# The gate stage of a four-layer convolution kernel, rewritten as one hand-ordered stream over rows of 8x8 blocks

## The chip, the cores and the metric

The kernel runs on one core of a Trainium2 chip. The metric is the device time of one launch in microseconds (us), as a median over runs. The core has five engines that work side by side and meet through semaphores: TensorE (PE, matrix products; its weight loads are listed as PEld), VectorE (DVE), ScalarE (ACT, functions by table), GpSimd (POOL) and SyncE (SP, which here only issues DMAs). Each takes its own instructions strictly in the order in which they stand.

## The reference

The input `x` is (2, 128, 128, 128) in float32: two images of 128 channels, 128 rows and 128 columns. Four layers follow each other. Layer 0 and layer 2 are a 3x3 convolution, a small state-space scan over every pixel, a group norm and a residual. Layer 3 is a basic block of two convolutions with signs as weights. Layer 1, which the change is about, is this:

```python
g = x.reshape(B, GROUP, c, hh, WINDOW, ww, WINDOW)          # GROUP = 4, c = 32, WINDOW = 8
g = g.transpose(0, 1, 3, 5, 2, 4, 6).reshape(B * GROUP * hh * ww, c, 64)
sq = jnp.sum(g * g, axis=-1)
gram = jnp.einsum('ncw,ndw->ncd', g, g)
dist2 = jnp.maximum(sq[:, :, None] + sq[:, None, :] - 2.0 * gram, 0.0)
density = jnp.exp(-0.5 * dist2).mean(axis=-1)               # one value per channel and 8x8 block
y = jax.nn.relu(einsum('bchw,oc->bohw', density, w1) + b1)  # 128 -> 32 channels
y = einsum('bchw,oc->bohw', y, w2) + b2                     # 32 -> 128 channels
attn = upsample_bilinear_ac(jax.nn.sigmoid(y) + 0.5, 8)     # 16x16 blocks -> 128x128 pixels
return x * attn
```

So each 8x8 block of each channel is compared with the same block of the 32 channels of its group, the densities make a gate for each block and channel, and the gates, spread bilinearly over the pixels, multiply `x`. An output row needs the gates of the block rows just above and below it.

## The kernel before

The three stages that matter stand one behind the other: `_mamba` for layer 0, `_gates`, and `_mamba` for layer 2. Channels (or states) lie on the 128 partitions.

`_mamba` issues its work by hand: every piece gets a due time, the pieces are sorted, and they are recorded inside `tc.manual_schedule`, so each engine's order is that of the list. Its scan over tokens (L451, L469, L478, L479, L483) takes most of the program's time. It writes its output `y`, not yet normalised, to DRAM, and statistics of it to `stats`.

`_gates` goes over the 32 slabs of 8 rows (16 for each image b), each 128 x 1024 elements. The scheduler of the language decides each engine's order there, from the order of the source and its own priorities. `_norm` turns the statistics of both images into a scale and a shift, ahead of all slabs. Then, for a slab:

- `load` (L633, L635): two DMAs of 512 KB bring `y` and the layer's input; ACT applies SiLU (L636), POOL adds both in a block order, giving `x` (L638), which stays in SBUF in one of 21 buffers (`nh + 5`).
- `turn`: eight transposes on PE (L652) into PSUM tile `pt`; DVE copies it to `xt` (L654), ACT squares it to `xq` (L656) and squares `x` to `sq` (L659); DVE sums and scales to `nsq` (L661, L662).
- `density`: PE forms the Gram matrices in PSUM tile `pg` (L671 with `xq`, then L681 with `xt`); DVE adds `nsq` (L689), POOL clamps (L695), ACT takes the exponential (L696).
- `total`: DVE sums to `dens` (L700).

When all 16 slabs of an image have their `dens`, `gain(b)` makes the gates of the whole image: PE (L707), ACT ReLU (L709), and four times PE (L717, L718), ACT sigmoid (L719) and DVE add (L720). Only then can `apply` run for that image, slab by slab: PE spreads the gates over the pixels (L738), from gates that lie in four groups of 32 partitions, `k // 2` choosing the group, so two neighbouring segments mostly share one; DVE multiplies with `x` (L747), in two pieces where a segment boundary cuts the slab; ACT's queue issues the store (L751). The loop interleaves one `apply` of image 0 with one `turn` of image 1; the 16 applies of image 1 come behind everything.

In PSUM, one tag (`pt`, two buffers of three banks) serves `turn`, `apply` and `gain`, and `pg` has one buffer of two banks. The first instruction of layer 2 is a memset of its row band (L193), whose SBUF space the gate stage used, so it waits for the last store of the gate stage; then come the band's load (L198) and the convolution (L328).

The functions that the diff touches and their callers:

Of the kernel before, what the change touches and what calls it, by code (L numbers as in the profile page):

```python
# [31 lines left out]
P = 128  # L32
# [59 lines left out]
def _place(k):  # L92


    q = k // 2
    return k % 2 + 2 * (q // 4), q % 4


def _upsampling(H):

    _, fy = _bilinear(H)
    ix, fx = _bilinear(P)
    wx = np.zeros((P // WIN, P), np.float32)
    wx[ix, np.arange(P)] = 1.0 - fx
    wx[ix + 1, np.arange(P)] += fx
    segs = _segments(H)
    up = np.zeros((4, 2, P // WIN, 4, max(e - a for _, a, e in segs), P), np.float32)
    for k, a, e in segs:
        n, g = _place(k)
        for h in range(a, e):  # L110
            up[g, 0, :, n, h - a] = (1.0 - fy[h]) * wx
            up[g, 1, :, n, h - a] = fy[h] * wx
    return up.reshape(P, 4, -1)
# [488 lines left out]
def _gates(tc, src, w, con, y, stats, wm, b1, up, dst, H):  # L602

    nc = tc.nc
# [3 lines left out]
    nwin = nh * nw  # L608
    segs = _segments(H)
    with tc.tile_pool(name="dg", bufs=2) as dp, tc.tile_pool(name="dg1", bufs=1) as sp, tc.tile_pool(  # L610
        name="ps_t", bufs=2, space=PSUM
    ) as pst, tc.tile_pool(name="ps_g", bufs=1, space=PSUM) as psg:

        def wide():
            return pst.tile([P, 3 * ROWS, P], F32, tag="pt", name="pt")

        class Small:


            def tile(self, shape, dtype, tag=None, name=None):  # L620
                return wide().rearrange("p a b -> p (a b)")[: shape[0], : shape[1]]

        norm = [_norm(nc, sp, Small(), w, con, stats, b) for b in range(B)]
        ct = sp.tile([P, 4, up.shape[2]], F32, tag="ct", name="ct")

        dens = [sp.tile([P, nh, 2, npair], F32, tag=f"dens{b}", name="dens") for b in range(B)]
        held, live, gains = {}, {}, {}

        def load(b, y0):

            rows = slice(y0 * WIN, (y0 + 1) * WIN)
            g = dp.tile([P, WIN, P], F32, tag="g", name="g", bufs=4)
            nc.sync.dma_start(out=g, in_=y[b][:, rows, :])  # L633
            xr = dp.tile([P, WIN, P], F32, tag="xr", name="xr", bufs=4)
            nc.sync.dma_start(out=xr, in_=src[b][:, rows, :])  # L635
            nc.scalar.activation(g, g, AF.Silu, bias=norm[b][1], scale=norm[b][0])  # L636
            x = held[b, y0] = dp.tile([P, nw, WIN, WIN], F32, tag="x1", name="x1", bufs=nh + 5)
            nc.gpsimd.tensor_tensor(by_row(x), by_row(xr, False), by_row(g, False), ALU.add)  # L638
# [6 lines left out]

        def turn(b, y0):

            x = held[b, y0].rearrange("p x r w -> p (x r w)")

            pt = wide()[:, :npair, :]  # L650
            for k in range(npair):
                nc.tensor.transpose(pt[:, k, :], x[:, k * P : (k + 1) * P], con["ident"])  # L652
            xt = dp.tile([P, npair, P], F32, tag="xt", name="xt")
            nc.vector.tensor_copy(xt, pt)  # L654
            xq = dp.tile([P, npair, P], F32, tag="xq", name="xq")
            nc.scalar.activation(xq, pt, AF.Square)  # L656

            sq = dp.tile([P, nw, WIN * WIN], F32, tag="sq", name="sq", bufs=1)
            nc.scalar.activation(sq.rearrange("p x r -> p (x r)"), x, AF.Square)  # L659
            nsq = dp.tile([P, nw], F32, tag="nsq", name="nsq")  # L660
            nc.vector.tensor_reduce(nsq, sq, AX.X, ALU.add)  # L661
            nc.vector.tensor_scalar_mul(nsq, nsq, -0.5)  # L662
            live[b, y0] = xt, xq, nsq

        def density(b, y0):
            xt, xq, nsq = live.pop((b, y0))

            pg = psg.tile([P, 2, 512], F32, tag="pg", name="pg")
# [19 lines left out]
            kk = dp.tile([P, 2, npair, CG], F32, tag="kk", name="kk", bufs=3)  # L688
# [6 lines left out]
            nc.gpsimd.tensor_scalar_min(kk, kk, 0.0)  # L695
            nc.scalar.activation(kk, kk, AF.Exp)  # L696
            live[b, y0] = kk

        def total(b, y0):
            nc.vector.tensor_reduce(dens[b][:, y0], live.pop((b, y0)), AX.X, ALU.add)  # L700

        def gain(b):

            den = sp.tile([P, nh, npair, 2], F32, tag="den", name="den")
            nc.vector.tensor_scalar_mul(den, dens[b].rearrange("p y a k -> p y k a"), 1.0 / CG)
            p1 = wide().rearrange("p a b -> p (a b)")[:CG, :nwin]
            nc.tensor.matmul(p1, lhsT=wm["w1"], rhs=den.rearrange("p y k a -> p (y k a)"), start=True, stop=True)  # L707
            hid = sp.tile([CG, nwin], F32, tag="hid", name="hid")
            nc.scalar.activation(hid, p1, AF.Relu, bias=b1)  # L709
            p2 = wide()[:, :4, :]  # L710
            gt = gains[b] = sp.tile([P, 4, P], F32, tag="gain", name="gain")
            for n in range(4):
                at = (n % 2 + n // 2 * WIN) * nw
                m = min(P, nwin - at) // 32 * 32
                if m <= 0:
                    continue
# [39 lines left out]
        for n in range(-4, N + 2):  # L756
            if ready:
                apply(*ready.pop(0))
# [237 lines left out]
```

## Time and profile before

| | us |
|---|---|
| median of 9 runs | 7870.99 (7850.73 to 7903.14) |
| time of the profiled execution | 7870.99 |
| its span in the trace | 7869.2 |
| busy PE / DVE / ACT / POOL over the span | 6556.4 / 6837.2 / 4291.1 / 5518.9 |
| last scan output of layer 0 on DVE (L511) | 3321.2 |
| first transpose of the gate stage (L652) | 3341.85 |
| last transpose of the gate stage | 3560.8 |
| last multiplication (L747) begins | 3638.3 |
| memset of layer 2's band (L193) | 3643.28 |

The page's busy shares are means over stages of different kinds. The gate stage is about 320 us of 7869, some 4% of the span, so it must be read from windows of its own. In a group's row, the first number behind the bar is busy time, the second the mean duration of one instruction in ns, and then follows the idle time of the engine just ahead of such instructions with what ended it. A row's `x` counts instructions; a float32 matmul appears as two. `PEclk` is the granted clock of TensorE as a share of full speed.

### The profile page before, as it was taken

The page shows a single profiled execution, that of the slowest core. Times are in us where ns is not written, and L with a number is a line of the kernel's source. Part 1 is how long each engine was busy: PE and PEld are TensorE (multiplying, and loading weights), DVE is VectorE, ACT ScalarE, POOL GpSimd, SP SyncE. Part 2 cuts the span into 40 slices and gives each one's busy share as a digit, 9 for nine tenths or more (in the row PEclk, how much of TensorE's full clock was granted, in tenths as well). Part 3 has the DMA queues.
Part 4 walks back from the last instruction along what each step waited for, and adds up shares of the span by engine and source line. Part 5 has one row for each costly group of instructions (what it writes and reads, how often), then busy time and mean ns, then how long its engine had stood idle before and what let it go on. Part 6 is the DMA issues. An engine that isn't in the chain of part 4 may idle for free. (4 is left out here: it accounts for less than half of the span.)

```text
span 7869.2 us, 86792 instructions
## 1 busy us (share of the span) xinstructions
PE 6556.4 (83%) x29412; PEld 2221.6 (28%) x29412; DVE 6837.2 (87%) x6360; ACT 4291.1 (55%) x4835; POOL 5518.9 (70%) x1810
## 2 busy tenths in 40 slices
PE   7888888888888888778888888888888888878893
PEld 2222222222222222253222222222222222223341
DVE  5999999999999999863999999999999999963454
ACT  5566565666666656482656666666666656621112
POOL 5777877777778778552777777777777778843330
PEclk8999999999999999766999999999999999989996
DMA  7999999999999999753999999999999999955204
GB/s 197 244 252 248 255 249 247 251 253 248 253 250 250 250 244 256 210 181 124 244 251 249 251 249 247 250 249 247 253 250 246 249 250 251 250 157 139 69 0 163
DMA packets 573435, 1765.42 MB, mean 224 GB/s; under 512 B 85536, under 2 KB 239680, under 8 KB 458176
## 3 DMA queue, kind: packets, MB, share of 16 engines
q1 hardware_dynamic: 530496, 1709.54, 84.0%
q10 hardware_dynamic: 42496, 50.34, 1.8%
q8 instruction: 234, 3.83, 0.2%
q14 instruction: 209, 1.71, 0.1%
HBM read 1549.82 MB, written 209.72 MB: 224 GB/s over the span
## 5 line engine op out<-in xcount | busy, mean ns | idle before, releaser
L451 POOL TENSOR_TENSOR h<-ur,bcr 128x2048 f32<-128x2048 f32 x896 | 4059.6, 4537 | 1273.0 <-DMA bcr<-sb 1058.2
L478 DVE TENSOR_TENSOR set<-set,h 128x1024 f32<-128x1024 f32 x1792 | 2194.3, 1224 | 308.3 <-ACT set L469 303.6
L479 DVE TENSOR_TENSOR r<-set,bcr 128x1024 f32<-128x1024 f32 x1792 | 2194.5, 1225 | 61.5
L469 ACT ACTIVATE set<-set 128x1024 f32<-128x1024 f32 x1792 | 1745.7, 1007 | 866.1 <-PE set L460 851.7
L483 DVE TENSOR_TENSOR h<-set,h 128x1024 f32<-128x1024 f32 x1536 | 1866.1, 1215 | 22.3 <-POOL h L451 22.1
L460 PE MATMUL set<-dt,rep 32*128 32x512 f32 x7168 | 1406.5, 676 | 100.2 <-DVE h L483 94.2
L498 PE MATMUL ys<-r,ct 128*32 128x512 f32 x7168 | 1173.2, 636 | 35.5 <-DVE r L479 35.3
L328 PE MATMUL one<-band,conv 128*128 128x512 f32 x2304 | 1085.7, 608 | 24.0 <-DMA band<-in_x_dram 11.6
L828 PE MATMUL m<-comb,u 128*128 128x512 f32 x1536 | 689.5, 610 | 88.6 <-DVE Y L842 52.1
L406 PE MATMUL one<-xc,keep 128*64 128x512 f32 x1024 | 330.0, 728 | 468.0 <-ACT xc L363 362.6
L460 PEld LDWEIGHTS set<-dt,rep 32*128 32x128 f32 x7168 | 406.2, 193 | 998.5 <-issue 465.5
L328 PEld LDWEIGHTS one<-band,conv 128*128 128x128 f32 x2304 | 408.3, 190 | 673.9 <-issue 598.9
L489 PE MATMUL ys<-t,ct 128*128 128x512 f32 x512 | 325.8, 723 | 251.7 <-DVE v L511 250.2
L357 ACT ACTIVATE xc<-one,keep 128x512 f32<-128x512 f32 x256 | 176.0, 688 | 518.2 <-PE one L355 513.4
L498 PEld LDWEIGHTS ys<-r,ct 128*32 128x32 f32 x7168 | 181.1, 112 | 933.7 <-issue 764.2
L828 PEld LDWEIGHTS m<-comb,u 128*128 128x128 f32 x1536 | 297.1, 195 | 480.2 <-issue 457.7
L426 PE MATMUL one<-prod,ct 128*128 128x512 f32 x512 | 284.8, 639 | 114.5 <-POOL prod L418 78.0
L355 PE MATMUL one<-y,w_in 128*128 128x512 f32 x512 | 343.7, 760 | 5.8 <-ACT xc L357 3.1
L380 POOL TENSOR_TENSOR u<-dt,xc 128x1024 f32<-128x1024 f32 x128 | 302.7, 2365 | 51.1 <-ACT dt L374 51.1
L469 ACT ACT_TABLE_LOAD x252 | 323.3, 1283 | 4.5
L370 PE MATMUL one<-xc,w_dt 128*128 128x512 f32 x512 | 316.7, 703 | 4.1 <-ACT bc L413 4.1
L433 POOL TENSOR_TENSOR t<-t,xc 128x1024 f32<-128x1024 f32 x128 | 302.4, 2362 | 10.0
(136 smaller groups left out, 5751.1 us busy)
## 6 DMA issues: line engine op xcount, KB each, us to landing
ur<-su SPq DMA_DIRECT2D x896, 896.0 KB, 11.6
bcr<-sb SPq DMA_DIRECT2D x896, 448.0 KB, 11.8
ur<-su SPq DMA_DIRECT2D x896, 128.0 KB, 11.2
su<-u SPq DMA_DIRECT2D x1024, 64.0 KB, 3.1
sb<-bc SPq DMA_DIRECT2D x256, 224.0 KB, 2.8
bcr<-sb SPq DMA_DIRECT2D x896, 64.0 KB, 11.1
y<-o SPq DMA_DIRECT2D x128, 256.0 KB, 9.5
band<-in_x_dram SPq DMA_DIRECT2D x28, 640.0 KB, 10.9
```

Source lines behind the costliest of these rows:

```text
L328: nc.tensor.matmul(py.rearrange("p (r w) -> p r w", r=ROWS), lhsT=w["conv"][:, tap, :], rhs=xb[:, r + kh : r + kh + ROWS, kw : kw + P], st ...
L355: nc.tensor.matmul(p, lhsT=w[("in", "z")[i]][:, g, :], rhs=s["y"], start=True, stop=True)
L406: nc.tensor.matmul(p[g * NQ * DS : (g + 1) * NQ * DS, :], lhsT=w[("xb", "xcm")[i]], rhs=s["xc"][:, g, :], start=True, stop=True,)
L451: nc.gpsimd.tensor_tensor(b, s["ur", t], s["bc", t][:, 0].unsqueeze(1).to_broadcast([P, NJ, NS]), ALU.mult)
L460: nc.tensor.matmul(a[j // 2][:, j % 2, :], lhsT=w["rep"][r, q, :], rhs=s["dt"][r, g, :], start=True, stop=True, tile_position=(r.start, 0),)
L469: nc.scalar.activation(x, x, AF.Exp)
L478: nc.vector.tensor_tensor(pt, pt, s["h", t - 1][:, js, :], ALU.mult)
L479: nc.vector.tensor_tensor(s["r", t][:, js, :], pt, s["bc", t - 1][:, 1].unsqueeze(1).to_broadcast([P, 2, NS]), ALU.mult)
L483: nc.vector.tensor_tensor(s["h", t][:, js, :], pt, s["h", t][:, js, :], ALU.add)
L489: nc.tensor.matmul(s["ys", g], lhsT=con["ident"], rhs=s["t1"][:, g, :], start=True, stop=False)
L498: nc.tensor.matmul(s["ys", g][a : a + NQ * DJ, :], lhsT=red[:, q, :], rhs=r[:, j, :], start=False, stop=(q == NQ - 1), tile_position=(0, a),)
L828: nc.tensor.matmul(m[:, i], lhsT=u[:, i, kw, :], rhs=v[:, i, :, kw : kw + P], start=(kw == 0), stop=(kw == 2),)
```

## The change

`_gates` is rewritten as one stream over the 32 slabs, inside `tc.manual_schedule`. The source loops over steps n, and in step n every piece of work is issued for slab n minus its own distance ("lag"). The whole-image gate is gone. A slab's `hide` makes the hidden values of its own row of 16 blocks and puts them in a row of `hidden[b]`, `gate` makes the gates of four rows of blocks at once (twice, in partitions 0 to 63 and 64 to 127), the sigmoid is ACT's exponential with a sum, a reciprocal and a sum on DVE (128 x 128), and `spread` fills a slab with two matmuls of 64 x 512, one from each half of the partitions. The multiplication is one instruction for a slab. The store moves from ACT's queue to SP's. The second image's `_norm` is issued in step 10, in front of that step's `gram`, instead of ahead of the stage. The upsampling constant grows from 128 x 4608 to 128 x 8192 elements. `x1` has 15 buffers instead of 21; `pt` has two of two banks; `pg`, `one` and `two` have one each. SiLU and POOL's addition are issued two slabs at a time, as are the loads.

```diff
+            s["xt"] = dp.tile([P, npair, P], F32, tag="xt", name="xt")
+            nc.vector.tensor_copy(s["xt"], pt)
+            s["xq"] = dp.tile([P, npair, P], F32, tag="xq", name="xq")
+            nc.scalar.activation(s["xq"], pt, AF.Square)
+            s["sq"] = dp.tile([P, nw, WIN * WIN], F32, tag="sq", name="sq")
+            nc.scalar.activation(s["sq"].rearrange("p x r -> p (x r)"), x, AF.Square)
...
-            den = sp.tile([P, nh, npair, 2], F32, tag="den", name="den")
-            nc.vector.tensor_scalar_mul(den, dens[b].rearrange("p y a k -> p y k a"), 1.0 / CG)
-            p1 = wide().rearrange("p a b -> p (a b)")[:CG, :nwin]
-            nc.tensor.matmul(p1, lhsT=wm["w1"], rhs=den.rearrange("p y k a -> p (y k a)"), start=True, stop=True)
-            hid = sp.tile([CG, nwin], F32, tag="hid", name="hid")
-            nc.scalar.activation(hid, p1, AF.Relu, bias=b1)
...
+        def hide(b, y0):
+            s = live[b, y0]
+            s["ph"] = psg.tile([CG, nw], F32, tag="one", name="ph")
+            nc.tensor.matmul(
+                s["ph"], lhsT=wm["w1"], rhs=s.pop("den").rearrange("p a k -> p k a"), start=True, stop=True
+            )
+
+        def hide_relu(b, y0):
+            nc.scalar.activation(hidden[b][:, y0 + 1, :], live[b, y0].pop("ph"), AF.Relu, bias=b1, scale=1.0 / CG)
+
+        def gate(b, y0):
+            s = live[b, y0]
+            p = s["pz"] = psg.tile([P, P], F32, tag="two", name="pz")
+            h = hidden[b][:, y0 : y0 + 4, :].rearrange("p y x -> p (y x)")
+            for a in range(0, P, P // 2):
+                nc.tensor.matmul(p[a : a + P // 2, :], lhsT=h, rhs=wm["w2"], start=True, stop=False)
+                nc.tensor.matmul(p[a : a + P // 2, :], lhsT=wm["one"], rhs=wm["b2"], start=False, stop=True)
+
+        def gate_exp(b, y0):
+            s = live[b, y0]
+            s["e"] = dp.tile([P, P], F32, tag="e", name="e")
+            nc.scalar.activation(s["e"], s.pop("pz"), AF.Exp, scale=-1.0)
+
+        def gain(b, y0):
+            e = live[b, y0]["e"]
+            nc.vector.tensor_scalar_add(e, e, 1.0)
+            nc.vector.reciprocal(e, e)
+            nc.vector.tensor_scalar_add(e, e, 0.5)
+
+        def spread(b, y0):
+            s = live[b, y0]
+            pu = s["pu"] = pst.tile([P, 2 * ROWS, P], F32, tag="pt", name="pu")
+            for n in range(2):
+                q = slice(n * P // 2, (n + 1) * P // 2)
+                nc.tensor.matmul(
+                    pu[:, n * ROWS : (n + 1) * ROWS, :].rearrange("p r w -> p (r w)"),
+                    lhsT=s["e"][q, :],
+                    rhs=weights[q, y0, :],
+                    start=True,
+                    stop=True,
+                )
...
+        stages = (
+            (3, density),
+            (6, hide_relu),
+            (8, gate_exp),
+            (1, norms),
+            (2, distance),
+            (0, turn),
+            (4, total),
+            (9, gain),
+            (10, apply),
+            (10, keep),
+            (1, gram),
+            (7, gate),
+            (5, hide),
+            (9, spread),
+        )
+        E = mybir.EngineType
+        with tc.manual_schedule(engines={E.PE, E.Activation, E.DVE, E.Pool, E.SP}):
+            for n in range(-6, N + 11):
+                if n % 2 == 0:
+                    for m in range(max(n + 4, 0), min(n + 6, N)):
+                        load(*order[m])
+                    for m in range(max(n + 2, 0), min(n + 4, N)):
+                        residual(*order[m])
+                for lag, stage in stages:
+                    if stage is gram and 0 <= n + 6 < N and order[n + 6][1] == 0:
+                        b = order[n + 6][0]
+                        norm[b] = _norm(nc, sp, psg, w, con, stats, b)
+                    if 0 <= n - lag < N:
+                        stage(*order[n - lag])
```

## The prediction

> **What bounds the kernel now.** I read the page first: DVE is busy 87% of the span, PE 83%, but both shares come from the two scan stages, which the change leaves alone. So I cut the gate stage out with windows: loading and first slabs, the part in which image 0 is also spread, and the rest in which only image 1 is spread.
>
> ```profile
> core 0: us, PE busy (x) PEld busy (x) DVE busy (x) ACT busy (x) POOL busy (x), PEclk, DMA share, GB/s
> ...
> 3342.00:3452.00 110.00, 66.08 (x2592) 53.74 (x2592) 71.19 (x85) 106.64 (x102) 70.46 (x36) 0.72 0.62 212
> 3452.00:3576.00 124.00, 107.44 (x2378) 67.74 (x2378) 82.60 (x106) 68.55 (x74) 49.70 (x27) 0.68 0.37 129
> 3576.00:3643.00 67.00, 58.52 (x106) 29.32 (x106) 21.33 (x28) 2.85 (x6) 0.00 (x0) 0.50 0.33 134
> ```
>
> Three limits follow each other. For 110 us ACT is busy 97%: 18 transposes in 110 us, 6.1 us a slab. For 124 us PE is busy 87%, 14 slabs at 8.9 us. For the last 67 us nothing but PE and DVE works, in turns, at half clock. The chain of waits for the second window, then two rows of it for the third:
>
> ```profile
> DVE o L747 <- PE pt L738: 16.0, 11, 3.2
> PEld pt L652 <- DVE o L747: 15.6, 6, 3.0
> ```
>
> ```profile
> POOL band L193 <- DMA x<-o: 70.7, 1, 70.7
> DVE o L747 <- PE pt L738: 34.2, 18, 4.1
> ```
>
> Multiplication and spread alternate through the two PSUM buffers; in the tail DVE waits 34.2 us for PE, and the next layer (POOL's band) waits for the last store. The tail exists only because an image's gates wait for its last density. The groups of the second window give the durations at its clock:
>
> ```profile
> L738 PE MATMUL pt<-ct,gain 32*128 32x512 f32 (+3 forms) x88 | 44.8, 636 | 2.3 <-DVE o L747 2.2
> ...
> L681 PE MATMUL pg<-xt 64*32 64x32 f32 x1920 | 24.7, 230 | 2.0 <-issue 2.0
> ...
> L652 PE MATMUL pt<-ct,x 128*128 128x128 f32 x112 | 23.7, 373 | 9.3 <-DVE o L747 8.6 <-ACT xq L656 0.7
> ...
> L671 PE MATMUL pg<-xq,ct 64*32 64x256 f32 x240 | 16.9, 566 | 1.8 <-DVE kk L689 1.8
> ```
>
> Per slab on PE: transposes 23.7/14 = 1.69 us, L671 16.9/15 = 1.13, L681 24.7/15 = 1.65, spread 44.8/16 = 2.8.
>
> **The change part by part.** The sum starts at ACT's first L656, at 3345.3 before, and ends with the last L747, at 3638.6 before. The profiled run took 7870.99 us, the median of the nine runs, 1.8 us more than its span; I subtract from both alike. What follows is counted from the order of the instructions on each engine.
>
> *Start.* The g loads lose a wait: SP stood 5.3 us at the load of `keep` (L235, for the second image's norm), with all loads queued behind; it now comes after the first store. But the constant ahead of them grows from 2304 KB, which took 8.5 us, to 4096 KB: 12 to 15 us from 3321.3, estimated at that rate and at the 440 GB/s of its best moments. Before its first squares ACT now also takes SiLU of slabs 2 and 3, so it waits for seven loads of 512 KB, 1.25 us each at that rate. Start: 3345, within 3 us. The second norm overlapped the first before; now it stands in step 10, between `apply` and the next sum on DVE and between `turn` and `gram` on PE. The whole chain took 3326.0 to 3331.8 for both; I charge 5.5 us.
>
> *Table loads.* SiLU two at a time and exponentials otherwise: 14 loads for SiLU and 15 for the exponential where the page has 21 and 22, and none for the sigmoid (3). One takes 1.283 us. ACT per slab: 1.24 (SiLU) + 1.01 + 1.05 + 0.63 + 1.28 (one load a slab) + 0.28 (L719's row, for the new exponential) + 0.2 (ReLU on 32 x 16, the 0.20 of L208) = 5.7 us.
>
> *Steps 0 to 8* (nothing is spread). ACT sets them: 9 x 2.06 (two squares), 8 SiLU 9.9, 6 exponentials 3.8, 7 table loads 9.0, the rest 1: 42 us; with 3 for waits, 45.
>
> *Spread on PE.* Before, 88 instructions for 16 slabs, mostly in one group of 32 rows, one behind the other. Now four for a slab, two in each half of the rows. The scan shows what row groups do:
>
> ```profile
> 3282.21 1.14 PE L460 MATMUL set<-dt,rep 32*128 32x512 f32 x8
> ...
> 3570.11 3.77 PE L738 MATMUL pt<-ct,gain 32*128 32x512 f32 x4
> ```
>
> Eight of the same size in four row groups took 1.14 us, where four in turn took 3.77 (at half clock; 1.89 at 3565). The row at half clock in row groups is 2.08 (3309.97). So 1.1 to 2.1, and 2.5 (4 x 0.636) if the halves do not overlap; I take 1.6. The Trainium skill, "TensorEngine Tiling (Array Packing)", Key Properties, speaks against it: changing the tiling mode drains the array, and each step here changes among full, 64 x 32, 64 x 64 and 64 x 128. The trace has such changes too (L652 to L671: 3506.01 after 1.90 us of transposes), and no gap beyond 0.3 us stands there; I add nothing. Four changes at 0.3 would add 1.2 us a step.
>
> *Gates.* Eight instructions of 128 columns and two of 16. L717 and L718 ran four in 1.2 us at half clock; in two column halves 0.85 to 2.4 for the eight, I take 0.9, and 0.1. PE per step: 1.69 + 1.13 + 1.65 + 1.0 + 1.6 = 7.1 us.
>
> *DVE.* The new gain: two sums of 128 x 128 (L720, median 0.23) and a reciprocal. The trace has reciprocals of 128 x 1 only (L209, 160 ns, against 155 of L207). From below: L747's row of 128 x 128, 0.28. From above: the skill's "VectorE: DVE Perf Modes" (Walkthrough) says that the reciprocal divides iteratively with a repeat count of 8; 128 x 8 at its 0.96 GHz is an estimated 1.07, with a fixed part 1.2. One column cannot tell these apart. I take 1.2; with 0.28 the step's loop below is 0.9 shorter, and the PE sum (7.1) rules: 11 us less in all.
>
> These operations also meet POOL:
>
> ```profile
> 3405.03 2.37 POOL L638 TENSOR_TENSOR x<-xr,g 128x1024 f32<-128x1024 f32 x1 [1.25 <-ACT g L636]
> 3405.79 1.64 DVE L662 TENSOR_SCALAR nsq<-nsq 128x16 f32<-128x16 f32 x1
> ```
>
> A scaling of 16 columns, 174 ns in the median, lasts until POOL's addition ends. Its mean is 490 and its maximum 2377: about 0.3 us each. "SBUF — State Buffer" (two separate sides) has the rule: a shared port pair is held for a whole instruction. By the mean, two sums add 0.6 a step; by the rule's worst, each waits 2.37. DVE per step: 1.22 + 1.22 + 0.49 + 0.69 + 0.68 + 0.46 + 1.2 + 0.6 + 1.22 = 7.8 by durations, some 7.1 since a following instruction starts up to 0.09 early.
>
> *Steps 9 to 31.* The lags take most waits out, but one loop is left. From the waits, `spread` takes the PSUM buffer that the same step's `turn` filled, so it waits for the copy `xt` and for `xq`, and it waits for `gain`, which stands behind `xt` and `total` on DVE; the next `turn` stands behind `spread` on PE. Loop: 1.69 + 1.22 + 0.68 + 0.46 + 1.2 + 0.6 + 1.6, and 0.2 for semaphores = 7.6 us. That is above the sums of PE (7.1), DVE (7.1) and ACT (5.7), so a late `gain` holds back `spread`, and behind it on PE every transpose. 23 steps: 175 us.
>
> *Tail.* Steps 32 to 41: one with `gram`, about 6 us, six with gates and spread at half clock (1.2 + 2.1), three shorter at 2.6: 33 us, where the old tail took 62.6. Spreads then alternate in the two buffers, so DVE and PE overlap.
>
> *Stores.* Their issue goes from ACT to SP, 0.33 us each behind a wait for `apply`; behind it are loads that have two steps (15 us) against 7.6 to land. They get late by part of a step at most. Without that slack a late store would move loads one for one. POOL's clamp now stands behind two additions (4.7 us) in every second step; its reader comes a step later. The last store lands after 4.7 us as before, and layer 2's band waits for it as before.
>
> Sum: 3345 + 45 + 175 + 5.5 + 33 = 3603.5 against 3638.6: 35 us less. Span 7834, median 7836.
>
> **The rivals.** (1) PE runs warmer. The clock was 0.68 in the second window with PE held up by DVE in between; if the closer stream brings full speed (transposes were 1.09 at 3391), the step falls to 6.2, by ACT and DVE: 23 x 1.4 = 32 us less, 7804. For it: 0.94 in the scan. Against: 0.72 and 0.68 in the gate stage, both with PE far from idle. (2) The distance is only on paper: PE stays at half clock (transposes 1.97, Gram 2.75, gates 1.3, spread 2.5, with drains) and the loop adds its waits, 8.9 us a step as before. Then only head, fill and tail gain: 23 x 1.3 = 30 us back, 7866. (3) Slower: the port. In every second step POOL runs two additions and a clamp back to back, some 6.2 us, and each of the two sums, perhaps the reciprocal too, can fall into it and wait up to 2.37. All sit on the loop. It decides from 9.1 us a step (35/23 = 1.5 over 7.6); at 10.4, 1.4 us more in each of two operations, it gives 23 x 2.8 - 35 = 29 us more, 7900. Against it: L662's median is the undisturbed 174 ns.
>
> **How the numbers follow.** 0.3% (24 us) is about what a measurement of this kernel can tell from no change. Forecast 0.60, 7 to 8.2 us a step, 7822 to 7850, a tenth of it above 7847; rival 1 0.22; rival 2 0.11; rival 3 0.07. Faster 0.54 + 0.22 = 0.76, same 0.06 + 0.11 = 0.17, slower 0.07. The range goes from 7798 (6.2 a step with a shorter start and tail) to 7866: it leaves out part of rivals 1 and 2, and 3.
>
> **What would show it.** Right: transposes 7 to 8 us apart in steps 9 to 31, spreads of four in 1.1 to 2.1, PE waiting at `spread` for `gain`, ACT's table loads at 29, last multiplication near 3603. Wrong: a reciprocal far from 1.2, sums of 128 x 128 above 1 us in the mean (rival 3), a clock above 0.9 (rival 1), spreads above 2.5, or a span that differs outside the gate stage by over 10 us.

## The result and the profile after

The changed kernel took 7851.92 us in the median of its first 11 runs (7834.58 to 7871.27), against 7870.38 for the kernel before in the same comparison: a ratio of 0.9975, with a 95% interval of 0.9963 to 0.9987. Repeated beside other kernels it gave 0.9965 (0.9952 to 0.9977). So it is faster by a quarter to a third of one per cent, 19 to 27 us, where 35 were predicted; the 24 us that the prediction took as the least that can be told from no change lie between the two. Its profiled span is 7844.1 us, 25.1 less.

Between profiles the end of layer 0, which no kernel here touches, lies anywhere from 3307.6 to 3335.5 us. What follows is therefore measured inside one trace, as the length of the stage: from layer 0's last scan output on DVE (L504 of the changed kernel, L511 before) to the memset of layer 2's band (L186, before L193). Before it was 3643.28 - 3321.23 = 322.1 us; after, 3616.35 - 3320.22 = 296.1 us, and 295.1 in the repeat. Such lengths come from one profile of each kernel.

The stage again in windows. The columns are those of the prediction's first fence: window and length, busy us (and instructions) of PE, PEld, DVE, ACT and POOL, granted clock, DMA share, GB/s. The windows are the steps before anything is spread, steps 9 and 10, the steady steps, and the tail:

```profile
3341.00:3398.00 57.00, 31.31 (x1249) 25.96 (x1250) 30.85 (x37) 41.81 (x46) 35.61 (x18) 0.80 0.61 222
3398.00:3425.40 27.40, 16.41 (x337) 10.80 (x337) 16.26 (x34) 15.24 (x20) 10.77 (x7) 0.50 0.28 104
3425.40:3579.00 153.60, 115.08 (x3488) 77.52 (x3486) 139.26 (x187) 105.56 (x141) 71.64 (x38) 0.89 0.49 181
3579.00:3614.00 35.00, 28.41 (x248) 12.43 (x246) 28.31 (x45) 4.69 (x15) 2.97 (x2) 0.55 0.37 151
```

In the third row DVE is busy 91% of the time, PE 75%, and PE's clock is 0.89 where the longest window before had 0.68. The tail is 35 us instead of 67, with DVE and PE both busy 81% of it: they overlap now. In the second row no engine is busy for more than 60% of the time: 27 us for two steps, at half clock.

The chain of waits for the third row:

```profile
DVE xt L648 <- PE pt L646: 13.9, 9, 3.9
...
PE pg L678 <- issue: 9.6, 8, 2.0
PE pg L668 <- DVE kk L690: 9.3, 12, 0.8
...
PE pu L745 <- DVE e L737: 6.2, 6, 2.1
```

DVE waits for one thing only, the transposes, 13.9 us in nine places; PE waits in turn for DVE's gain and distance, and 9.6 us for nothing that this view shows ("issue"; the repeat below names it). For the fourth row, the waits that answer to the last two lines shown before:

```profile
POOL band L186 <- DMA x<-o: 30.6, 1, 30.6
...
DVE o L756 <- PE pu L745: 4.3, 5, 1.1
```

DVE's 34.2 us of waiting for the spread have become 4.3. The band still waits for the last store, but for 30.6 us and not 70.7. The groups of the steady steps (21 of them):

```profile
L745 PE MATMUL pu<-up,e 64*128 64x512 f32 x86 | 30.6, 786 | 11.2 <-DVE e L737 6.2 <-ACT sq L652 5.0
L678 PE MATMUL pg<-xt 64*32 64x32 f32 x2688 | 29.8, 202 | 9.6 <-issue 9.6
...
L646 PE MATMUL pt<-ct,x 128*128 128x128 f32 x168 | 28.7, 327 | 0.0
...
L736 DVE RECIPROCAL e<-e 128x128 f32<-128x128 f32 x21 | 20.0, 953 | 0.7
...
L668 PE MATMUL pg<-xq,ct 64*32 64x256 f32 x336 | 15.7, 434 | 9.3 <-DVE kk L690 9.3
...
L737 DVE TENSOR_SCALAR e<-e 128x128 f32<-128x128 f32 x21 | 12.6, 601 | 0.7
...
L735 DVE TENSOR_SCALAR e<-e 128x128 f32<-128x128 f32 x21 | 9.4, 450 | 0.0
```

The reciprocal costs 0.953 us. The two sums take 0.450 and 0.601 in the mean, where the shortest of each takes 0.216 and 0.226: waits for the port of 0.23 + 0.37 = 0.6 us a step.

From turn to turn, the fill (first xq to step 9) took 51.7 us, step 9 12.6, step 10 15.0, and steps 11 to 31 7.35 each, (3572.32 - 3425.39)/20. That mean hides a pattern of two. A step in which ACT takes two SiLUs and POOL two additions (the even ones) lasts 8.0 us, the other 6.5 (medians; 7.6 and 6.5 in the repeat). Most experiments below are read in this pair.

The trace shows what an even step waits for (starts and durations in us; the lines between are left out):

```profile
3495.11 4.70 POOL L637 TENSOR_TENSOR x<-xr,g 128x1024 f32<-128x1024 f32 x2 [8.36 <-ACT g L635]
...
3497.03 0.55 DVE L735 TENSOR_SCALAR e<-e 128x128 f32<-128x128 f32 x1
...
3497.62 0.95 DVE L736 RECIPROCAL e<-e 128x128 f32<-128x128 f32 x1
...
3498.60 1.29 DVE L737 TENSOR_SCALAR e<-e 128x128 f32<-128x128 f32 x1
...
3499.76 1.50 POOL L696 TENSOR_SCALAR kk<-kk 128x512 f32<-128x512 f32 x1
```

POOL's two additions end near 3497.5 and at 3499.81. The first sum is released by the one (0.55 instead of 0.22), the second by the other (1.29, ending at 3499.89). The reciprocal between them runs beside an addition at its full speed.

### The profile page after: what moved, and what is told of

The parts are those of the page before. It is cut to its first block, busy times and chain, and to the rows that moved or that the text cites. A ratio compares the mean times of both kernels' runs of the same rounds, so it can differ in the third digit from the quotient of the medians.

```text
span 7844.1 us, 87434 instructions
## 1 busy us (share of the span) xinstructions
PE 6499.7 (83%) x29648; PEld 2198.1 (28%) x29648; DVE 6873.4 (88%) x6432; ACT 4279.4 (55%) x4873; POOL 5519.6 (70%) x1812
## 5 line engine op out<-in xcount | busy, mean ns | idle before, releaser
L491 PEld LDWEIGHTS ys<-r,ct 128*32 128x32 f32 x7168 | 180.5, 112 | 928.5 <-issue 762.1
L420 ACT COPY t<-one 128x512 f32<-128x512 f32 x256 | 150.0, 586 | 306.7 <-PE one L419 306.6
```

What stands on the lines that cost most here:

```text
L491: nc.tensor.matmul(s["ys", g][a : a + NQ * DJ, :], lhsT=red[:, q, :], rhs=r[:, j, :], start=False, stop=(q == NQ - 1), tile_position=(0, a),)
```

## The experiments

All ran on the chip beside the kernel before; "ratio" is to that kernel, and "step" the mean of steps 11 to 31.

**The changed kernel once more.** No edit.

> The changed kernel once more, for the times of this chip and as the trace that the others are read against. In the first profile of it the stage, from layer 0's last scan output on DVE (L511) to the memset of layer 2's band (L186), took 296.1 us (3320.22 to 3616.35; before 322.05), the fill (first xq to the transposes of step 9) 51.7, step 9 12.6, step 10 15.0, the steps after it 7.35 each and the tail 35. Expected: the same within 3 us in each part, a ratio of 0.9963 to 0.9987. PE stood without a recorded reason ('issue') for 3.60 us within L678 in step 9 and for 2.67 in step 19. If such a stop belongs to the program it comes back at the same place and length; if it is a matter of chance (say, of how instruction fetches meet the data transfers), it comes at other places with a like sum, some 22 us in the stage.

7842.87 us, ratio 0.9965. Stage 295.1, fill 52.3, step 9 10.6, step 10 15.05, step 7.36. PE's stops came back at the same places, within 3 us of stage time; most of the later ones had the same length, while that of step 9 was 2.03 instead of 3.60. In the gate (first profile, then repeat):

```profile
3483.86 0.47 PE L725 MATMUL pz<-w 32*64 32x128 f32 x1 [2.67 <-issue]
```

```profile
3472.42 0.45 PE L725 MATMUL pz<-w 32*64 32x128 f32 x1 [2.66 <-issue]
```

The places of these stops belong to the program, and the trace shows what PE waits for. From 3341 to 3612 us of the first profile PE has 10,689 records of matmuls and weight loads, and a DMA queue of the kind "instruction" moved 41 packets of 16 KB, one for about 260 records (packets, MB, share of the time of 16 DMA engines):

```profile
q8 instruction: 41, 0.67, 1.0%
```

Counted in these records, the eleven stops above 0.8 us of the first profile stand 256 or a multiple of 256 apart, to within one record, and each ends 1.1 to 1.5 us after such a packet has landed. The packet for the stop in the gate travelled from 3481.56 to 3482.47; PE had stopped at 3481.19 and went on at 3483.86. So PE stands at these places because its next instructions come late.

**Distance ahead of norms.**

```diff
-            (1, norms),
             (2, distance),
+            (1, norms),
```

> distance is issued ahead of norms in a step, on DVE and nothing else. Theory: in the fill the Gram matrices of a slab wait for the distance of the slab before (one pg buffer), and the distance stands on DVE behind the sums of squares of the following slab, which wait for ACT's sq behind two SiLUs (six such waits of PE, 15.3 us, up to 7.0 in one). With the distance in front the fill falls from 51.7 to 44-47 us; in the steady steps the waits of PE for the distance (9.3 us in 12) go, but DVE is busy 91% there, so that is worth 0 to 0.2 us a step. In all 5 to 10 us less. Rival: ACT's squares, SiLUs and table loads set the fill by themselves (41.8 us busy in its 57); then the fill stays above 50 and nothing is gained.

7849.98 us, ratio 0.9974 (0.9963 to 0.9984). The fill went from 52.3 to 50.4, not to 44-47, and step 9 from 10.6 to 6.5. The step grew from 7.36 to 7.96, which neither theory expected; stage 301.8. The cause is in the trace:

```profile
3467.96 4.67 POOL L637 TENSOR_TENSOR x<-xr,g 128x1024 f32<-128x1024 f32 x2 [7.04 <-ACT g L635]
...
3468.07 2.27 DVE L659 TENSOR_SCALAR nsq<-nsq 128x16 f32<-128x16 f32 x1
```

The scaling of 16 columns used to end just before POOL began. Moved back behind the distance, it begins 0.1 us after POOL in every even step and lasts until POOL's first addition ends. The even step went to 9.9 us, the odd one stayed at 6.5.

**The reciprocal left out.**

```diff
             nc.vector.tensor_scalar_add(e, e, 1.0)
-            nc.vector.reciprocal(e, e)
             nc.vector.tensor_scalar_add(e, e, 0.5)
```

> The reciprocal L736 is left out (the gate is then 1.5 plus the exponential). Theory: DVE sets the steady step (busy 139.3 of 153.6 us) and the reciprocal takes 0.953 us of it, so a step falls from 7.35 to about 6.4, 20 us over steps 11 to 31, and the tail by less than 5: 20 to 25 us less in all, ratio to the kernel before about 0.9945. Rival: PE with its stops, its waits and its clock is as close a bound (busy 115 of 153.6, and 38 us of stops and waits); then DVE's time turns into waiting for the transposes, and a step falls by 0.4 or less, under 9 us in all.

7849.53 us, ratio 0.9966 (0.9949 to 0.9982): nothing gained. Both theories are wrong, since the step grew to 7.77, stage 300.0. In the pair: the odd step fell from 6.5 to 5.8, three quarters of the reciprocal, and the even step grew from 7.6 to 10.3:

```profile
3511.07 4.67 POOL L637 TENSOR_TENSOR x<-xr,g 128x1024 f32<-128x1024 f32 x2 [7.75 <-ACT g L635]
...
3512.07 1.44 DVE L735 TENSOR_SCALAR e<-e 128x128 f32<-128x128 f32 x1
...
3513.55 2.27 DVE L736 TENSOR_SCALAR e<-e 128x128 f32<-128x128 f32 x1
```

(L736 is the second sum here.) Without the reciprocal both sums wait, 1.44 + 2.27, and the second again ends with POOL's second addition. In an even step the end of the gain is set by POOL, with or without 0.95 us of DVE's work in between. The spread then began only after the following multiplication (six such waits of PE, 10.7 us); why is not settled.

**The spread from one half of the partitions.**

```diff
-                q = slice(n * P // 2, (n + 1) * P // 2)
+                q = slice(0, P // 2)
```

> Both matmuls of spread read the gates and the weights of partitions 0 to 63, so they lie in one row group (half of the gates are left out of the result). The spread of four instructions should go from 1.13 (2.08 at half clock) to about 1.9 (3.8). Theory 1, DVE sets the step: after gain DVE has apply, the sum of squares, its scaling and the distance to do, 3.3 us, while PE spreads and transposes in 2.2 to 4.0; 0.8 more at the full clock is covered, at half clock it is not: a step grows by 0 to 0.5 us, 0 to 12 us in all with the tail apart. Theory 2, the loop of the prediction (gain, spread, turn, copy) sets it: 0.8 to 1.7 a step more, 18 to 38 us. In the tail, where PE is at half clock and the steps are short, each step grows by up to 1.7 in both: 10 to 17 us.

7870.76 us, ratio 1.0004 (0.9991 to 1.0017), stage 336.2. The spread took 1.95 at the full clock and 3.75 at half clock:

```profile
3469.76 3.75 PE L745 MATMUL pu<-up,e 64*128 64x512 f32 x4 [2.14 <-DVE e L737]
3478.80 1.95 PE L745 MATMUL pu<-up,e 64*128 64x512 f32 x4 [0.47 <-ACT sq L652]
```

So two row groups nearly halve it (1.13 and 2.08). The step grew to 8.48, 1.1 us more, and the last step's turn to the last multiplication took 54.8 instead of 39.8. That is the second theory's range: the spread lies on the loop. This one part is worth 336.2 - 295.1 = 41 us, more than the whole change brings.

**POOL's addition left out.**

```diff
-            nc.scalar.activation(g, g, AF.Silu, bias=norm[b][1], scale=norm[b][0])
             s["x"] = dp.tile([P, nw, WIN, WIN], F32, tag="x1", name="x1", bufs=15)
-            nc.gpsimd.tensor_tensor(by_row(s["x"]), by_row(xr, False), by_row(g, False), ALU.add)
+            nc.scalar.activation(by_row(s["x"]), by_row(g, False), AF.Silu, bias=norm[b][1], scale=norm[b][0])
```

> POOL's addition of the residual (L637) is left out: ACT's SiLU writes x in the block order itself, and the layer's input, still loaded, is not added. Nothing of DVE's work is touched. What is to be told apart: in the changed kernel DVE's two sums of the gain (L735, L737; 0.22 us undisturbed) take 0.37 to 0.45 and 0.60 to 0.68 in the mean; leaving out the reciprocal (0.95 us of DVE a step) did not shorten the step but lengthened it from 7.36 to 7.77, and the two sums then took 0.78 and 1.13; putting distance before norms made the scaling L659 last 1.35 instead of 0.17, and the step 7.96. Theory 1: a TENSOR_SCALAR of DVE that falls under POOL's addition lasts until the addition ends, and this sets every second step. Then without the addition L735, L737 and L659 go back to 0.22, 0.23 and 0.17 (POOL's clamp, 1.5 us, may still hold some), and the step falls from 7.36 to 6.5-6.8: 11 to 17 us over 20 steps. Theory 2: the order of the waits on PE (spread, turn, gram at half clock) sets the step and the long sums only fill time in which DVE would wait; then the step stays within 0.2 of 7.36.

7817.08 us, ratio 0.9949 (0.9930 to 0.9967), stage 282.0. The groups of its steady steps (lines stand one higher):

```profile
L735 DVE RECIPROCAL e<-e 128x128 f32<-128x128 f32 x21 | 20.0, 953 | 0.7
...
L734 DVE TENSOR_SCALAR e<-e 128x128 f32<-128x128 f32 x21 | 4.7, 223 | 0.0
L736 DVE TENSOR_SCALAR e<-e 128x128 f32<-128x128 f32 x20 | 4.5, 226 | 0.7
```

Theory 1, nearly: the sums are undisturbed, and the step fell to 6.88 (6.5 to 6.8 were expected), 0.48 us less, 13 us in the stage; the even step went from 7.6 to 6.8. Without the addition POOL's clamp and the next slab's `x` come earlier too; a version below keeps the addition and takes the sums from DVE instead.

**The addition and the reciprocal left out.** Both diffs together.

> Both left out: POOL's addition of the residual as in the run without it, and DVE's reciprocal L736. Theory 1 (POOL's addition holds DVE's small operations and so hid the reciprocal): with the addition gone the reciprocal's 0.953 us count, and the step is 0.5 to 0.95 us shorter than without the addition alone, 5.8 to 6.2 us, where PE (5.5 us busy a step, and its stops) is the next bound. Theory 2 (PE sets the step): the same step as without the addition alone within 0.2 us.

7816.48 us, ratio 0.9939 (0.9922 to 0.9956), stage 282.5, step 6.90. Theory 1's second half falls: the reciprocal is worth nothing in the mean here either, though no addition covers it. The odd step fell from 6.4 to 5.7, the even one grew from 6.8 to 8.5. What holds the pair at 13.8 us must be something that spans both steps, and not POOL.

**No TENSOR_SCALAR on DVE.** The same result by other means:

```diff
-            nc.scalar.activation(s["e"], s.pop("pz"), AF.Exp, scale=-1.0)
+            nc.scalar.activation(s["e"], s.pop("pz"), AF.Tanh, scale=0.5)
+            nc.scalar.activation(s["e"], s["e"], AF.Copy, scale=0.5, bias=1.0)
...
-            (9, gain),
...
-            nc.scalar.activation(s["sq"].rearrange("p x r -> p (x r)"), x, AF.Square)
+            nc.scalar.activation(s["sq"].rearrange("p x r -> p (x r)"), x, AF.Square, scale=0.5**0.5)
...
-            nc.vector.tensor_scalar_mul(s["nsq"], s["nsq"], -0.5)
...
-                ALU.add,
+                ALU.subtract,
```

> A version that computes the same with no TENSOR_SCALAR on DVE in the stage: the gate is ACT's tanh of half the argument, and a second ACT instruction makes 1 + 0.5 tanh of it (L735, L736 and L737 are gone); the square for the norms is taken with scale sqrt(0.5), and distance subtracts (L659 is gone). DVE loses 2.0 + 0.17 us a step of its 6.66, ACT gains 0.26 of its 5.05 a step. Theory 1: the step falls to 5.8-6.3, where PE (5.5), ACT (5.3) and the loop turn, copy, xq, spread (1.07 to 1.97 + 1.22 + 1.0 + 1.13 to 2.08 = 4.4 to 6.3) are close together: 20 to 30 us less in steps 11 to 31 and some 5 in the tail, stage about 265, ratio to the kernel before about 0.993. Theory 2 (PE sets the step as it is): the step stays above 7.

7826.42 us, ratio 0.9946 (0.9929 to 0.9962), stage 278.3, step 6.80 with 8.4 and 5.8 in the pair. That lies between the two theories. DVE fell from 107 to 80 us of work in a window of 120, and the step by only 0.56:

```profile
3440.00:3560.00 120.00, 94.55 (x2853) 63.89 (x2854) 80.34 (x86) 96.33 (x141) 66.61 (x36) 0.87 0.60 211
```

DVE is no longer the bound; ACT and PE are the busiest, at 80 and 79%. PE's largest wait for another engine in an even step is before the gate:

```profile
PE pz L723 <- ACT e L729: 13.1, 8, 2.3
```

**One step more between ReLU and gate**, on top of the last version (gate_exp 9, apply and store 11, gate 8, spread 10; three buffers for `e`, 16 for `x1`).

> The version without TENSOR_SCALAR on DVE (step 6.80, DVE busy only 80 of 120 us there), with one step more between hide_relu and gate (gate 8, gate_exp 9, spread 10, apply and store 11), three buffers for e and 16 for x1. In that version, and in the one without POOL's addition, every second step still takes 8.4 to 8.9, and there PE stands before the gate (13.1 us in 8 waits of 120 us) for ACT's ReLU of the same step, which is queued behind two SiLUs, two table loads and an exponential. Theory 1: this wait is the bound that replaced DVE; with a step more it goes, and the step falls from 6.8 to 6.0-6.4 (PE 5.5 busy and 0.4 of stops; ACT 5.8), 8 to 16 us less than without it, one step of 3.7 more in the tail: stage 266 to 274. Theory 2: ACT's own work in the step with SiLUs (8.2 us) sets the pair, since the following copies and squares stand behind it; then the step stays within 0.2 of 6.8 and the stage grows by the longer tail.

7831.58 us, ratio 0.9940 (0.9921 to 0.9959), stage 278.7, step 7.03, nothing gained, close to the second theory. PE still stood 12.4 us in seven waits before the gate. I had named the wrong releaser. `pz` has one buffer, so a step's gate waits until the same step's gate_exp has read it, and that stands behind the SiLUs on ACT whatever the distance. The combined version below bears this out: with gate_exp in front of the SiLUs this wait is gone.

**The second norm in step -3.**

```diff
-                    if stage is gram and 0 <= n + 6 < N and order[n + 6][1] == 0:
-                        b = order[n + 6][0]
+                    if stage is gram and n in (-6, -3):
+                        b = (n + 6) // 3
```

> The second image's norm is issued in step -3, behind the loads of the first slabs and ahead of all of PE's work, instead of in step 10. Step 10 of the changed kernel took 15.0 us twice, where its neighbours take 7.36, so the norm costs 7.7 us there (5.5 were charged in the prediction). Theory 1: between loads and first transposes PE, DVE and ACT stand idle, so the norm is free there: step 10 falls to 7-8.5, the head (last scan output to first xq, 26.0 us) stays within 1, and the stage is 6 to 8 us shorter. Rival: the load of the statistics is late behind 4 MB of constants and four loads, so ACT's square root stands in front of the first SiLU and the head grows by 2 to 5 us, half of the gain or more.

7829.48 us, ratio 0.9950 (0.9937 to 0.9963). Step 10 fell to 6.5, 8.6 less, but the head grew from 26.0 to 29.4; stage 291.0, 4.1 us less. The rival was right about the size and wrong about the cause. SP's queue at the start of the stage:

```profile
3335.96 0.33 SPq L228 DMA_DIRECT2D keep<-in_L_keep_dram  x1
3336.39 0.37 SPq L627 DMA_DIRECT2D g<-y  x1
```

The next layer's load of `keep` waits for the end of the norm, and the first g load stands behind it.

**Without the load of the layer's input.**

```diff
-            s["xr"] = dp.tile([P, WIN, P], F32, tag="xr", name="xr", bufs=4)
-            nc.sync.dma_start(out=s["xr"], in_=src[b][:, rows, :])
...
-            g, xr = s.pop("g"), s.pop("xr")
+            g = xr = s.pop("g")
```

> The changed kernel without the load of the layer's input in the stage (L629); POOL adds g to itself, so that every engine has the same work and only the data transfers shrink by a third. What is asked: PE stops without a recorded reason ('issue') in the run of the changed kernel at the same places as in its first profile (25, 34, 59, 90, 112, 136 (in the gate, 2.66 us), 165 and 208 us after the first xq, with 1.4 to 2.9 us each, 17.8 us in the larger ones together), so they belong to the program. Theory 1: there PE has used up the instructions that were fetched, and the fetch waits among the data transfers; with a third fewer transfers the stops shrink, above all the two in the fill (1.82 + 2.89) and the one in step 9 (2.03), to under half in the sum, and the fill falls from 52.3 to 47-49 us. Theory 2: the fetch costs the same whatever else is transferred; then the stops keep their places and lengths within 20%, and the fill stays at 52 (the first xq comes earlier in both, by up to 7 loads x 1.25 / 2 = 4 us).

7836.19 us, ratio 0.9958 (0.9945 to 0.9972), stage 291.1. PE's stops kept their places; up to 210 us after the first xq they sum to 15.0 us, against 17.6 in the repeat of the changed kernel and 19.3 in its first profile. The one in the gate:

```profile
3466.12 0.32 PE L723 MATMUL pz<-w 32*64 32x128 f32 x1 [2.37 <-issue]
```

The fill stayed at 51.1. Theory 2, nearly: with a third less traffic the stops are 15 to 22% shorter in sum, where the two profiles of the changed kernel differ by 9%. The packets took about 1 us with and without that traffic; the one for the gate's stop set out 0.1 us after PE had stopped here.

**What the runs point to, together**: no TENSOR_SCALAR on DVE, both norms ahead of the stage, `e` in three buffers, and, on ACT, ReLU and gate_exp in front of a step's SiLUs:

```diff
+            for b in range(B):
+                norm[b] = _norm(nc, sp, psg, w, con, stats, b)
             for n in range(-6, N + 11):
+                for lag, stage in ((6, hide_relu), (8, gate_exp)):
+                    if 0 <= n - lag < N:
+                        stage(*order[n - lag])
                 if n % 2 == 0:
```

> What the runs point to, put together: no TENSOR_SCALAR on DVE (as in that version, stage 278.3, step 6.80), both norms ahead of the stage, and hide_relu and gate_exp issued ahead of a step's SiLUs on ACT instead of behind them (e has three buffers). In the version with one step more between hide_relu and gate the step did not fall (7.03), and PE still stood 12.4 us in 7 waits before the gate for ACT: pz has one buffer, so the gate of a step waits for the gate_exp of the same step, which is queued behind two SiLUs, two table loads and an exponential; the added distance did not touch that. Theory 1: with gate_exp in front of the SiLUs that wait goes, and the step falls to 6.0-6.4. Step 10 falls from 13.6 to 6-7. The head, 26.3 us, grows by 0 to 2: in the run with the norm in step -3 it grew by 3.4, because the load of the next layer's weights (keep) stands ahead of the first g loads on SP and waits for the end of that norm (3335.96); ahead of the stage the norm ends some 3 us earlier, as before the change (3332.16). Stage 257 to 266, ratio to the kernel before 0.990 to 0.993. Theory 2: ACT's 8.2 us in a step with SiLUs set the pair of steps whatever their order; then the step stays at 6.6 or above, stage 270 or more.

7802.74 us against 7846.55, ratio 0.9943 (0.9931 to 0.9955), stage 270.0: about as much again as the change itself brought. By its ratio it cannot be told from the version without TENSOR_SCALAR alone (0.9946); in the profile its stage is 8 us shorter. Step 10 fell to 6.2, the head grew by 3.1 (0 to 2 were expected), since the load of `keep` left 15.6 us after layer 0's last scan output, no earlier than with the norm in step -3 (15.4). From the last turn to the last multiplication 28.6 us passed instead of 36.9. But the steady step is 6.84, the second theory's side, and the ratio stays short of the 0.990 to 0.993 expected. The gate no longer waits for the exponential; instead these appear:

```profile
PE pg L667 <- DVE kk L689: 6.8, 5, 1.6
...
PE pt L646 <- ACT xq L650: 4.6, 4, 1.3
```

**Without the distance.** The stages in the order of one slab's data: turn, norms, gram, distance, density, total, hide and hide_relu with lag 0, and gate to store with lag 1.

> The same pieces without the distance: in a step everything is issued in the order of the data for one slab (turn, norms, gram, distance, density, total, hide, relu), and then gate to store for the slab before it, whose gate needs this slab's hidden row. Expected from the durations of the changed kernel's rows: a step is the chain turn 1.97, copy 1.22, xq 1.02, gram 1.10 + 1.57, distance 0.68, clamp 1.49, table load and exponential 1.28 + 0.63, total 0.67, hide 0.29, relu 0.25, gate 1.3, exponential 0.26, gain 1.4, spread 2.08: 18 us, with some 16 hand-overs at 0.1 to 0.2 about 20, less what overlaps at the end (the next turn needs only PE free and a PSUM buffer): 17 to 21 us a step, the stage 550 to 680 us instead of 296, 250 to 380 us more than with the distance, ratio to the kernel before 1.03 to 1.046. Rival: the distance does little, since each engine's queue is long and the pieces of neighbouring slabs overlap in any order; then a step stays under 11 us.

8091.85 us, ratio 1.0295 (1.0272 to 1.0318), stage 559.5, step 16.5: somewhat under the expected 17 to 21, and far from the rival's 11. The distance halves the stage. The kernel before, at 322, did overlap neighbouring slabs: in its second window a slab took 8.9 us, where the chain of one slab takes 16.5 here.

## Why the prediction was right, and where it was off

The time came out between forecast and rival 2: 7851.9 for a predicted 7836, inside the range, with the stage 25.9 us shorter for a predicted 35; the repeat, 7842.9, lies within the forecast itself. The mechanism held: each engine's work of several slabs overlaps, the tail halves, and the spread lies on the loop. The last multiplication ended 10 us later than the sum has it, at 3613.3 for 3603.5: start 1.1, fill 6.7, steps 9 to 31 with the norm 1.1 (181.6 for 180.5), tail 0.9. That steps 9 to 31 fit so well is luck: step 9 and the norm were put 7 us too low, and the other 21 steps 6 us too high.

*Start.* 3345 predicted, 3346.1 measured, though layer 0 ended one us earlier; from that end it is 25.9 for 23.8. SiLU's and the exponential's table loads were 14 and 15, as counted.

*Fill: the first term that was too small.* 45 us predicted, 51.7 measured. The sum of ACT's work, 42, was sound (39.2 us busy in these 51.7), the 3 us for waits were not. Two of PE's stops (2.37 and 2.62) fall there, and gram waits for the distance behind the norms (15.3 us in six waits). Undoing the second alone brought 1.9 us (50.4), less traffic 1.2 (51.1), and the version without TENSOR_SCALAR 3.1 (49.2), so which of them holds the fill is not settled.

*Step 9* took 12.6 instead of 7.6; 3.6 of it is one stop of PE. Nothing in the sum stood for such stops, though the trace of before had them in L681 (2.0 us in the prediction's own row).

*The norm* was put at 5.5 us; step 10 took 7.7 more than its neighbours, and 8.6 left it when the norm went. The chain of both norms in the idle head, 5.8 us, was the wrong row: in step 10 the chain stands behind queued work, and PE, where everything else of the step is queued behind it, waits for its first link on DVE:

```profile
3417.78 0.56 PE L582 MATMUL pm<-mv,ct 128*128 128x1 f32 x2 [5.44 <-DVE mv L579]
```

*Steady steps: right in size, 7.35 for 7.6, by a partly wrong loop.* The reciprocal took 0.953 (1.2 taken; the bounds were 0.28 and 1.2, and the upper one, estimated from the repeat count of 8 in the Trainium skill's "VectorE: DVE Perf Modes" (Walkthrough), was nearer). The waits for POOL cost 0.6, as taken. The spread was 1.13 to 2.08 (1.6 taken) with no gap for a change of mode. The clock was 0.89, not 0.68, and with it the turn 1.38 instead of 1.69. With the measured means the loop gives 1.38 + 1.22 + 0.68 + 0.46 + 0.62 + 0.95 + 1.39, and 0.2 for semaphores = 6.9 us. So its terms were 0.7 too long together, and what it left out made up for most of that; PE's stops alone are 12.2 us in 20 steps, 0.6 a step. The loop through gain, spread, turn and copy is confirmed for the spread: 0.8 to 1.7 us more in it cost 1.1 a step. For the reciprocal it fails: the loop counts every duration once, but in an even step the gain ends when POOL's additions end, and 0.95 us of DVE's work beneath them is free. The additions are not the whole reason: without them the reciprocal is worth nothing either (6.88 and 6.90). Odd and even steps should have been summed apart.

*Tail.* 33 predicted, 34 measured from the end of step 31's spread (3579.4). The memset came 3.0 us after the last multiplication, where 4.7 were taken.

*Rivals.* (1) had the clock nearly right (0.89, just under its sign of 0.9) and the step wrong: its 6.2 by ACT and DVE lies below the prediction's own 7.1 for DVE, which PE's clock does not touch, and was not reached even with DVE unloaded. How much of the shorter step is the clock's no run sets apart. (2) was wrong in its clock and in its step. (3), the port, acts as described, but where the kernel lies it takes 0.6 a step and not 2.8. How near it was, two runs show: moving a 0.17 us instruction by one place brings 2.1 us of port wait into each even step (2.27 - 0.17), taking the reciprocal away 3.3 in all (1.44 + 2.27, less 0.22 and 0.23).

*What holds the versions without port waits.* Five runs stay at 6.8 to 7.0 us a step, 13.6 to 14.1 a pair, whatever was taken from DVE or moved on ACT. In the version without TENSOR_SCALAR the trace shows a loop over two steps (ACT's rows, PE's rows between them):

```profile
3492.57 1.28 ACT L635 ACT_TABLE_LOAD   x1
3493.86 2.37 ACT L635 ACTIVATE g<-g,aff_t,aff_s 128x1024 f32<-128x1024 f32 x2
3496.25 1.28 ACT L699 ACT_TABLE_LOAD   x1
...
3498.54 0.44 PE L723 MATMUL pz<-w,hid 32*64 32x128 f32 x4 [2.29 <-ACT e L729]
...
3499.30 2.08 PE L745 MATMUL pu<-up,e 64*128 64x512 f32 x4
3501.30 1.73 PE L646 MATMUL pt<-ct,x 128*128 128x128 f32 x8
...
3504.33 1.02 ACT L650 ACTIVATE xq<-pt 128x1024 f32<-128x1024 f32 x1 [1.64 <-DVE xt L648]
...
3506.31 1.28 ACT L635 ACT_TABLE_LOAD   x1
```

From table load to table load 13.7 us pass: two table loads, two SiLUs and an exponential on ACT, then gates, spread and turn on PE, the copy on DVE, two squares on ACT. Followed back from step 30 to step 11 by what released what, the chain takes in both table loads of all nine pairs there; in the changed kernel itself it meets the first table load of only four (three in the repeat), and runs through DVE and POOL besides. In the combined version, where ReLU and gate exponential stand ahead of the SiLUs, it still takes in seven: there the turn waits for `xq`, and the distance for the sums of squares, both behind the SiLUs on ACT.

*What stays open.* No run takes the SiLUs apart, so what a step would be without this loop is not shown. Nor is there a run of the new order with the gates of a whole image: of the parts of the rewrite, only the distance and the two row groups were tested alone.

## What to carry to other kernels

Sum a software pipeline over the period in which its queues repeat, not over one step: here two steps, because SiLU and addition come in pairs. An operation is worth nothing where another engine's end releases the next one anyway, so before counting a saved microsecond, look which engine's end the following instruction meets. Small DVE instructions that wait for POOL, as TENSOR_SCALAR did here, should stand where POOL is idle, or be done on ACT; the long reciprocal stood beside POOL for nothing.

## What the runs showed of the hardware that I had not expected

- DVE's TENSOR_SCALAR from SBUF to SBUF waits for the end of POOL's addition and lasts up to 2.3 us for 0.17 us of work, while RECIPROCAL (953 ns, always within 952 to 955) and TENSOR_REDUCE (L706, 0.67 us) beside the same additions are not touched. The Trainium skill's "SBUF — State Buffer" (Who interferes with whom) says the first, and of the reduction the second; that the reciprocal escapes is this trace's.
- PE's stops without a recorded reason are waits for instructions. Of the 120 above 0.8 us in the stage, in all 14 profiles of this case, each stands at a multiple of 256 PE records from the others of its profile, to within one, and ends 0.9 to 1.6 us after a 16 KB packet of the instruction queue landed. They take up to 3.6 us in the changed kernel, 12.2 us in 20 steady steps. Not every packet brings a stop (eleven of 41 in the first profile). A third less data traffic changes them little; the order of other engines changes them more: with distance ahead of norms, and PE's own program the same, they sum to 12.0 us instead of 17.6, and the one in the gate to 0.20 instead of 2.66, where PE had just waited 1.88 us for ACT.
- Two matmuls of 64 rows in the two halves of the partitions take 1.13 us against 1.95 in one half, at half clock 2.08 against 3.75.
